# Rows of two, three and three batch elements in layer 1, and few-bit feed-forwards in halves

## The chip, the cores and the metric

The kernel runs on one core of one Trainium2 chip. A core has TensorE for matrix products, VectorE (DVE), ScalarE (ACT) and GpSimd (POOL) for everything elementwise, and SyncE (SP), whose queue issues nearly all DMAs here. Times are device microseconds of one execution; for a version the median of several executions counts, and less is better.

## The reference, cut to what matters

Two layers work on `x`, 8 batch elements of 512 tokens with 256 channels, and on a context of 512 tokens with 128 channels. Each layer adds to `x` a gated attention part and a gated feed-forward part, each on a normalised `x`.

- Layer 0, attention: causal self-attention and cross-attention over the context, 16 heads of 16 channels, then a projection.
- Layer 0, feed-forward: `h = gelu(qlinear(x, W1))`, `out = qlinear(h, W2)`, where `qlinear` quantises its input to 8 bits with one scale for the whole tensor. The second one needs the smallest and the largest `h` of all batch elements before any of them can go on.
- Layer 1, attention: two transformer blocks one after the other, `a1` (self-attention; the mask comes after the softmax and keeps keys later than the query) and `a2` (attention over the context). Both have 16 heads of 32 channels, and each has an MLP of its own, 256 to 1024 to 256:

```python
o = softmax(q k^T / sqrt(32)) (* mask) @ v
x_out = x + o @ li1_w + li1_b
h = gelu(_ln(x_out) @ li2_w + li2_b)
return x_out + h @ li3_w + li3_b
```

- Layer 1, feed-forward: activations quantised to 8 bits with a scale for each token, weights to three values, and between the two products a convolution over three tokens for each channel and a SiLU: `bit_linear(silu(conv(bit_linear(x, w1))), w2)`.

## The kernel before

Everything of batch element `b` stays with tokens or channels on the 128 partitions. The work is given out by a planner while the program is built. `Pace` (line 745) notes every instruction that is recorded, with a cost from a table (`cost`, line 863), and so keeps for each engine the time at which it should be free. The pieces of work are Python generators wrapped as `Stream`: each yields `need(...)`, the tiles that it waits for next, and whether its next piece starts on TensorE. [...]A helper records all matmuls on line 1022 and all transposes on line 1025.

Layer 0's attention, and its first feed-forward product, come first (up to about 910 us). What the second product needs is stored to memory: `hd`, 1 MB for each batch element. Layer 1 then is one long weave, `layer1_xattn` with `weave_all` (line 1762). Its parts:

- **Attentions** (`steps1`, line 2120): 16 of them, called slots here, in the order `order`. Before, the batch elements go in pairs: (0, a1), (1, a1), (0, a2), (1, a2), (2, a1), and so on. A slot has 4 head groups of 4 steps. A step's `front` makes the scores of four heads for 128 keys into two PSUM tiles `ps_s` and their exponentials into `pt` on ScalarE (line 2146); for a1, GpSimd selects the diagonal block into `dg` (line 2150). Its `back` multiplies with the values into the single bank `ov`. VectorE sums the exponentials into `acc` (lines 2175 and 2177). At the end of a group, VectorE turns the sums into reciprocals and scales `ov` into `oT` (lines 2190 to 2195), and only then can the next group's first `back` use `ov`. At most two fronts are ahead of the backs.
- **`pre1`** (line 1939): two normalisations in front of a1, the transposed `zT`, and the values `vt`. **`pair1`** (line 2011): queries and keys of one head group; for a2 the keys come from memory (`kd`), where they were put earlier.
- **`mlp1`** (line 2031): for each half of 256 tokens: output projection `li1`, normalisation, MLP with `li2`, Gelu (line 2093) and `li3`. After a1 its end prepares the same batch element's a2 (`enter1`). The half 0 of a1's MLP also loads a2's values into `vt` (line 2080).
- **`first`** (line 1856): the second product of layer 0's feed-forward, in two halves of 256 tokens: load `hF`, scale and round on ScalarE (line 1883), clip and subtract on VectorE (lines 1885 and 1887), 16 matmuls.
- **`last`** (line 2215): layer 1's feed-forward of one batch element, for which a2's MLP must be done. In each half, eight times: one product, `hp` (line 2249), then the convolution on `hF` (lines 2252 to 2261); then SiLU (line 2265), the largest magnitude of each token (`hm`, line 2269), a scale from it through two small TensorE groups, `hF*sr` and its rounding into `hq` (lines 2284 and 2286), 16 matmuls.
- **`tail`** (line 2315): the same feed-forward for the last batch element, each half by itself, with the convolution on TensorE.

Each stream has a `base`, the slot number at which it is due, and a `share`, by which its due time grows as its work gets done. `weave_all` takes, among the pieces that can start by the time TensorE should be free, the one that is due first. A piece that doesn't start on TensorE is recorded once its tiles are ready and VectorE's planned end is no more than `lag` ahead of TensorE. `first` and `last` form one list, sorted by base: `first` of the batch elements 0 to 7 is due at -1, 0, 1, 2, 3, 4, 7, 8, `last` of 0 to 6 at 5, 6, 9, 10, 13, 14, 15.

MLP weights have one buffer each. A new set is loaded when both halves of the second element of a pair have used the old one (`used`, line 1829), and a stream waits in `weight` until the set of its pair is in.

Of the kernel before, what the change touches and what calls it, by code (L numbers as in the profile page):

```python
# [8 lines left out]
F32 = mybir.dt.float32  # L9
BF16 = mybir.dt.bfloat16  # L10
AF = mybir.ActivationFunctionType
ALU = mybir.AluOpType
AX = mybir.AxisListType
PSUM = bass.MemoryType.PSUM

P = 128
B, T, C, CC = 8, 512, 256, 128
H = 16
NT = T // P
# [5 lines left out]

MAGIC = 12582912.0
NEG = -1.0e30
PTS = 3
KEYS_FIRST = 6

# [714 lines left out]
class Pace:  # L745
# [117 lines left out]
    def cost(self, e, ins, outs, srcs):  # L863
        size = self.size

        op = str(ins.opcode)
        n = max(size(a) for a in outs + (srcs if "Reduce" in op else []))

        few = sum(size(a) == 1 for a in srcs)
        if e == "PE":  # L870
            start = 0.0 if self.groups is None else 0.19
            if ins.is_transpose:
                return start + 0.095
            return start + n * (0.00169 if srcs[0].dtype == F32 else 0.00042)
        if e == "Activation":
            f = str(getattr(ins, "func", "Copy")).rsplit(".", 1)[-1]
            sbuf = srcs[0].tensor.space != PSUM
            t = n * 0.00084 + 0.16
            if f == "Identity":
                t += 0.22 if sbuf else 0.09 * few  # L880
            elif f == "Gelu" and n <= T:
                t += 0.19
            if f in ("Exp", "Gelu", "Silu") and f != self.table:
                self.table = f
                t += 1.28
            return t
        psum = any(a.tensor.space == PSUM for a in outs + srcs)
        two = sum(size(a) == n for a in srcs) > 1
        if e == "Pool":
            if "Affine" in op:  # L890
                return 0.25 + n * 0.001
            return 1.05 if n <= 2 * NT and two else 0.22 + n * 0.0021
        if "Reduce" in op:
            return 0.14 + n * (0.00173 if len(srcs[0].ap) > 2 and list(srcs[0].ap)[-1][0] > 1 else 0.00106)
        if "BNStats" == op:
            return 0.41
        if n <= 4 * NT:
            return 0.17
        if psum or two or "Transpose" in op:
            return 0.15 + 0.05 * few + n * 0.00106  # L900
        return 0.15 + 0.05 * few + n * 0.0006
# [2 lines left out]
WAIT = object()  # L904


def need(*tiles, pe=True, room=()):


    return [Pace.name(t) for t in tiles], pe, room  # L910


class Stream:
# [27 lines left out]
class Fast(General):  # L941
# [94 lines left out]
    def weave_timed(self, ops, streams, drain=False):  # L1036

        pace, behind = self.pace, self.behind  # L1040
        ops = list(ops)
        n_ops, i = len(ops), 0
        live = list(streams)

        def advance(s):
            w = pace.work
            s.need = next(s.gen, None)
            s.done += pace.work - w
            if s.need is None:
                s.over = True  # L1050
                if s in live:
                    live.remove(s)

        def starts(s):
            names, on_pe, room = s.need
            t = max([pace.when(names)] + [pace.place(tag) for tag in room])
            return max(t, pace.place("m1")) if on_pe else t

        while i < n_ops or live or (drain and not behind.over):
            now = pace.free.get("PE", 0.0)  # L1060
            cands = []
            for s in live + ([] if behind.over else [behind]):
                while s.need is WAIT:
                    last = s.need
                    advance(s)
                    if s.need is WAIT:
                        break
                while not s.over and s.need is not WAIT and not s.need[1] and starts(s) <= now:
                    advance(s)
                if s.over or s.need is WAIT:  # L1070
                    continue
                cands.append((s.base + s.share * s.done / s.total, starts(s), s))
            if i < n_ops:
                cands.append((i / n_ops, ops[i][0](), None))
            if not cands:
                continue
            can = [c for c in cands if c[1] <= now + 0.3]
            pick = min(can, key=lambda c: c[0]) if can else min(cands, key=lambda c: (c[1], c[0]))
            if pick[2] is not None:
                advance(pick[2])  # L1080
            else:
                ops[i][1]()
                i += 1
# [624 lines left out]
    def layer1_xattn(self):  # L1708
        nc, tc = self.nc, self.tc
        with (  # L1710
# [16 lines left out]

            self.pairs = self.fronts = self.backs = self.zTs = self.nvt = 0
            self.li1s, self.mlps, self.loads, self.both_in = [0, 0], [0, 0], {}, {}
            order = [(2 * p + k, blk) for p in range(B // 2) for blk in range(2) for k in range(2)]  # L1730
            few, pairs, mlps, pres = [], [], [[], []], [[], []]

            for k, b in zip((-1, 0, 1, 2, 3, 4, 7, 8), range(B)):
                few.append(Stream(self.first(b), 3.8, 0.8, k, 1.0))
                if b == 1:
                    few.append(Stream(self.load_mlp(), 1.0, 1.0, k))
            for k, b in zip((5, 6, 9, 10, 13, 14, 15), range(B - 1)):
                few.append(Stream(self.last(b), 10.5, 0.8, k, 1.0))
            few.sort(key=lambda s: s.base)
            for k, (b, blk) in enumerate(order):  # L1740
# [6 lines left out]
            for half in range(2):  # L1747
                mlps[half][-1].base += 0.4 * half
                mlps[half].append(Stream(self.tail(half), 20.0, 1.0, 17 + 0.4 * half))
            self.final, self.tails = {}, [0, 0]  # L1750
            diag = [Stream(self.diagonals(), 1.0, 0.1, 15.5)]
            self.keys_done, self.x0_read = False, 0
            keys = [Stream(self.keys2_rest(), 8.0 * (B - KEYS_FIRST), 1.0, -1.0)]
            self.weave_all(
                [self.steps1(b, blk) for b, blk in order], [few, pairs, *mlps, *pres, diag, keys]
            )
            self.pace.close()

# [3 lines left out]
    def weave_all(self, attns, chains):  # L1762
# [12 lines left out]
                c.pop(0)  # L1775

        def starts(s):
            names, on_pe, _ = s.need
            t = max(pace.when(names), pace.free["DVE"] - s.lag)
            return max(t, pace.place("m1")) if on_pe else t  # L1780

        while self.backs < len(steps) or any(chains):
# [39 lines left out]

    def weight(self, name, b, blk):

        while self.loads.get(name) != self.slot_of(b, blk) // 2:
            yield WAIT
        return self.wl[name]

    def used(self, name, b, blk):

        if self.both(b, (name, blk)) and b % 2 and (b, blk) != (B - 1, 1):
            self.next_weight(name, 1 - blk)

    def few_weights(self, layer, names):
# [21 lines left out]
    def first(self, b):  # L1856
# [22 lines left out]
        for half in range(2):  # L1879
            if half:  # L1880
                h = h2 or load_h(1)
            yield need(h, pe=False)
            nc.scalar.activation(h, h, AF.Identity, scale=self.rh, bias=self.magic)
            yield need(h, pe=False)
            nc.vector.tensor_scalar(h, h, self.hlo, self.hhi, ALU.max, ALU.min)
            hq = work.tile([P, NF, n], BF16, tag="hq", name="hq")
            nc.vector.tensor_scalar(hq, h, MAGIC, None, ALU.subtract)
            yield need(hq, x)
            ps = self.bank().rearrange("p (k c) -> p k c", k=2)
            for k in range(2):  # L1890
# [107 lines left out]

    def slot_of(self, b, blk):

        return 4 * (b // 2) + 2 * blk + b % 2

    def turned_half(self, z):

# [6 lines left out]
    def pair1(self, b, blk, g):  # L2011
# [15 lines left out]
            self.plus(KT, ps, w["wk_b"][:, g : g + 1])  # L2027
        q["QK", blk, g] = (QT, KT)
        self.pairs += 1

    def mlp1(self, b, blk, half):

# [37 lines left out]
        if blk:  # L2070
# [1 line left out]
            x = self.load_x(1, b, f"xo{half}", half)  # L2072
            yield need(res, x, pe=False)
            nc.vector.scalar_tensor_tensor(res, res, self.gate[:, 1:2], x, ALU.mult, ALU.add)
        elif not half:
            while self.nvt < self.slot_of(b, 1) or self.backs < 16 * (self.slot_of(b, 1) - 1):
                yield WAIT
            vt = q["vt", 1] = work.tile([P, NT, 2 * C], F32, tag="vt", name="vt", bufs=2)
            self.nvt += 1
            nc.sync.dma_start(vt.rearrange("p t c -> p (t c)"), self.vd[b])  # L2080
        li2 = yield from self.weight("li2", b, blk)
        h = work.tile([P, NF, n], F32, tag=f"hD{half}", name="hD")
        for f2 in range(NF // 2):
# [131 lines left out]
    def last(self, b):  # L2215
# [25 lines left out]
        for half in range(2):  # L2241
# [3 lines left out]
            for f in range(NF):  # L2245
# [14 lines left out]
                for k in (1, 2):  # L2260
                    nc.vector.scalar_tensor_tensor(  # L2261
                        a, hp[:, half + k : half + k + n], self.col("conv_w", 3 * f + k), a, ALU.mult, ALU.add
                    )
            yield need(h, pe=False)
            nc.scalar.activation(h, h, AF.Silu)
            yield need(h, pe=False)

            hm = work.tile([P, n], F32, tag="hm", name="hm")
            nc.vector.tensor_reduce(  # L2269
                hm, h.rearrange("p f t -> p t f"), AX.X, ALU.max, apply_absolute_value=True  # L2270
            )
            yield need(hm)
            ps = self.bank()[:, 0:n]
            for i in range(2):
# [5 lines left out]
            yield need(sc)  # L2280
            sr = work.tile([P, n], F32, tag="sr", name="sr")
            nc.scalar.copy(sr, self.row_of(sc, range(2)))
            yield need(sr, pe=False)
            nc.vector.tensor_tensor(h, h, sr.unsqueeze(1).to_broadcast([P, NF, n]), ALU.mult)
            hq = work.tile([P, NF, n], BF16, tag="hq", name="hq")
            nc.vector.tensor_scalar(hq, h, MAGIC, MAGIC, ALU.add, ALU.subtract)
            nc.vector.tensor_scalar(k, un, self.units["f1_w2"], self.gate[:, 3:4], ALU.mult, ALU.mult)
            yield need(hq, k, x)
            ps = self.bank().rearrange("p (k c) -> p k c", k=2)
# [236 lines left out]
```

## Time and profile before

Three executions took 2857.25, 2861.83 and 2867.59 us. The profile is of another execution.

| what | value |
|---|---|
| median of the three executions | 2861.83 us |
| profiled execution, its own time | 2859.76 us |
| its span, from the first to the last instruction | 2858.0 us |
| TensorE busy, matmuls | 2531.8 us (89%) |
| VectorE busy | 1708.6 us (60%) |
| ScalarE busy | 1453.9 us (51%) |
| GpSimd busy | 619.6 us (22%) |
| mean granted TensorE clock | 0.953 |
| moved by DMA | 181.79 MB, 64 GB/s |
| first score matmul of layer 1 | 964.1 us |
| last score matmul of layer 1 | 2695.4 us |

How to read it: the profile cuts the span into 40 equal slices and gives the busy share of each engine in tenths, and the clock that the throttle granted to TensorE. A row of a group has its line, engine, operation, the tiles it writes and reads, shape and count, its busy time and the mean duration in ns. A wait is put down to the instruction that ended it. Since matmuls overlap and their ends are modelled, a busy TensorE is not one that works at its peak.

### The profile page before, as it was taken

To read this page: it belongs to the slowest core of one execution; us is meant where nothing else is said; L and a number is where in the kernel's file an instruction comes from. 1 tells how busy PE (TensorE), PEld (TensorE's weight loads), DVE (VectorE), ACT (ScalarE), POOL (GpSimd) and SP (SyncE) were. 2 spreads that over 40 slices of the span, in tenths; PEclk is the share of its full clock that TensorE was granted. 3 is DMA by queue.
4 is the path that set the end of the run, shared out by engine and by line. 5 is a ranking of instruction groups with operands and counts; after the bars stand their busy time and mean duration, and the time that the engine had idled before them with its cause. 6 is when DMAs were issued, how large, how long until landed. Compare 5 with 4: busy or idle time off the path is not lost.

```text
span 2858.0 us, 38403 instructions
## 1 busy us (share of the span) xinstructions
PE 2531.8 (89%) x15431; PEld 1227.1 (43%) x15436; DVE 1708.6 (60%) x3014; ACT 1453.9 (51%) x1802; POOL 619.6 (22%) x693
## 2 busy tenths in 40 slices
PE   5999999999874888999999998999899999898875
PEld 2333333333232335445545444456354455353454
DVE  2434544344276555656656767766777755767766
ACT  3666666566574534544445544454554444554431
POOL 2112221121100333313332112132323112212010
PEclk9999999999987989999999999999999999998988
DMA  2011101100165421231220120131111020021010
GB/s 95 23 42 48 49 8 64 34 31 12 41 244 216 153 84 54 92 103 63 63 78 23 34 100 15 67 126 52 52 61 58 23 82 23 28 84 45 16 45 16
DMA packets 77338, 181.79 MB, mean 64 GB/s; under 512 B 7520, under 2 KB 36576, under 8 KB 69344
## 3 DMA queue, kind: packets, MB, share of 16 engines
q1 hardware_dynamic: 74768, 176.05, 17.6%
q8 instruction: 123, 2.02, 0.3%
q0 software_dynamic: 800, 2.62, 0.3%
q10 hardware_dynamic: 1584, 0.58, 0.1%
q14 instruction: 63, 0.52, 0.1%
HBM read 116.32 MB, written 62.91 MB: 63 GB/s over the span
## 4 chain that ended last, share of the span: by engine, by line
PE 67%; DVE 18%; ACT 7%; issue 4%; POOL 3%; DMA 1%; SPq 0%; ACTq 0%; POOLq 0%; DVEq 0%
PE ps L1022 38%; PE ps_s L1022 15%; PE ov L1022 12%; DVE hext L1636 2%; PE ps L1025 2%; ACT pt L1384 1%; POOL dg L2150 1%; DVE mv L1907 1%; ACT pt L2146 1%; DVE hF L2261 1%; DVE hm L2269 1%; DVE acc L2177 1%; DVE acc L2175 1%; DVE rb L2193 1%; ACT hD L2093 1%
## 5 line engine op out<-in xcount | busy, mean ns | idle before, releaser
L2146 ACT ACTIVATE pt<-ps_s 128x1024 f32<-128x1024 f32 x512 | 496.4, 1021 | 441.9 <-PE ps_s L1022 352.0
L1022 PE MATMUL ps_s<-QT,KT 32*128 32x512 f32 (+3 forms) x4096 | 618.0, 612 | 35.8 <-ACT pt L2146 12.2
L1384 ACT ACTIVATE pt<-ps_s 128x1024 f32<-128x1024 f32 (+3 forms) x512 | 411.6, 862 | 196.5 <-PE ps_s L1022 188.8
L1022 PEld LDWEIGHTS ps_s<-QT,KT 32*128 32x128 f32 x4096 | 193.7, 186 | 372.2 <-issue 202.0
L2150 POOL TENSOR_SCALAR_AFFINE_SELECT dg<-pt 128x512 f32<-128x512 f32 x128 | 121.3, 949 | 649.8 <-ACT pt L2146 649.7
L1022 PE MATMUL ov<-pt,v 128*32 128x512 f32 (+3 forms) x2048 | 235.3, 530 | 17.2 <-POOL pt L1387 14.1
L1022 PE MATMUL ps<-li,hD 128*128 128x256 f32 x1024 | 238.8, 389 | 12.1 <-ACT hD L2093 12.1
L1022 PE MATMUL ps<-x3T,li 128*128 128x256 f32 x1024 | 244.0, 390 | 1.4 <-ACT x3T L2063 1.1
L1022 PE MATMUL ov<-pt,vt 128*32 128x512 f32 (+3 forms) x1792 | 204.8, 525 | 39.4 <-DVE oT L2195 33.2
L1022 PEld LDWEIGHTS ps<-li,hD 128*128 128x128 f32 x1024 | 193.4, 193 | 66.1 <-issue 17.6
L1022 PEld LDWEIGHTS ps<-x3T,li 128*128 128x128 f32 x1024 | 192.0, 194 | 55.3 <-issue 15.3
L1387 POOL TENSOR_SCALAR_AFFINE_SELECT pt<-pt 128x512 f32<-128x512 f32 x128 | 86.4, 676 | 477.3 <-ACT pt L1384 477.3
L1913 POOL TENSOR_SCALAR mv<-mv 128x2 f32<-128x2 f32 (+1 forms) x105 | 51.2, 487 | 621.0 <-DVE mv L1908 560.9
L2177 DVE TENSOR_TENSOR acc<-acc,pt 128x2048 f32<-128x2048 f32 x64 | 151.9, 2374 | 8.2 <-ACT pt L2146 7.2
L2175 DVE TENSOR_TENSOR acc<-pt 128x2048 f32<-128x2048 f32 x64 | 149.7, 2339 | 0.6 <-ACT pt L2146 0.6
L1409 DVE STREAM_TRANSPOSE ot<-ov 128x512 f32<-128x512 f32 x64 | 45.8, 715 | 166.3 <-PE ov L1022 166.3
L1022 PE MATMUL ps<-zT,a_wq 128*128 128x512 f32 x256 | 135.4, 656 | 6.1 <-DVE zT L1994 4.1
L2261 DVE SCALAR_TENSOR_TENSOR hF<-hp,cols,hF 128x256 f32<-128x256 f32 x224 | 113.1, 505 | 34.6 <-ACT hF L2252 28.1
L1022 PE MATMUL ps<-li,oT 128*128 128x256 f32 x512 | 128.0, 395 | 1.6 <-DVE oT L2195 1.1
L1022 PEld LDWEIGHTS ov<-pt,v 128*32 128x32 f32 x2048 | 40.6, 108 | 174.9 <-issue 109.5
L1022 PEld LDWEIGHTS ps<-li,oT 128*128 128x128 f32 x512 | 94.0, 193 | 44.5 <-issue 16.4
L1025 PE MATMUL ps<-ident,z 128*128 128x128 f32 x328 | 60.9, 308 | 55.2 <-DVE z L137 34.5
(285 smaller groups left out, 3618.1 us busy)
## 6 DMA issues: line engine op xcount, KB each, us to landing
hd<-h SPq DMA_DIRECT2D x16, 1024.0 KB, 3.9
hF<-hd SPq DMA_DIRECT2D x16, 1024.0 KB, 6.7
li<-in_w_a_dram SPq DMA_DIRECT2D x16, 1024.0 KB, 5.0
fw<-q_f_w SPq DMA_DIRECT2D x22, 512.0 KB, 5.8
xF<-xd SPq DMA_DIRECT2D x22, 512.0 KB, 5.3
kd<-k SPq DMA_DIRECT2D x8, 1024.0 KB, 4.9
vd<-v SPq DMA_DIRECT2D x8, 1024.0 KB, 5.0
res<-rd SPq DMA_DIRECT2D x32, 256.0 KB, 2.7
```

The lines of the kernel that those rows point to most:

```text
L1022: self.nc.tensor.matmul(out, lhsT, rhs, start=start, stop=stop, skip_group_check=True)
L1025: self.nc.tensor.transpose(out, in_, self.ident)
L1384: nc.scalar.activation(pt[:, 2 * jp : 2 * jp + 2, lo:], pss[jp][:, :, lo:], AF.Exp)
L1387: nc.gpsimd.affine_select(out=diag, in_=diag, compare_op=ALU.is_ge, fill=0.0, base=0, pattern=[[0, 4], [1, P]], channel_multiplier=-1,)
L1409: nc.vector.transpose(ot.rearrange("p b d -> p (b d)"), ov)
L1636: nc.vector.tensor_reduce(e, hh, AX.X, op)
L1913: nc.gpsimd.tensor_scalar(rstd, mv[:, :, 1], EPS, None, ALU.add)
L2146: nc.scalar.activation(pt[:, 2 * jp : 2 * jp + 2, :], pss[jp], AF.Exp)
L2150: nc.gpsimd.affine_select(out=dg, in_=pt[:, :, diag], compare_op=ALU.is_gt, fill=0.0, base=0, pattern=[[0, 4], [-1, P]], channel_multiplier=1,
L2175: nc.vector.tensor_tensor(st["acc"], st["pt"], pt, ALU.add)
L2177: nc.vector.tensor_tensor(st["acc"], st["acc"], pt, ALU.add)
L2261: nc.vector.scalar_tensor_tensor(a, hp[:, half + k : half + k + n], self.col("conv_w", 3 * f + k), a, ALU.mult, ALU.add)
```

## The change

Three things are changed.

1. **Rows.** The pairs become the rows `ROWS`: (0, 1), (2, 3, 4) and (5, 6, 7). Each row runs a1 for all its elements and then a2 for all of them. So slots 0 to 5 stay as they are, ending with (2, a1) and (3, a1); then come (4, a1), (2, a2), (3, a2), (4, a2), (5, a1), (6, a1), (7, a1), (5, a2), (6, a2), (7, a2). `slot_of` and the weights' waits follow the rows; there are six sets of MLP weights to load in place of eight. The load of a2's values leaves `mlp1` and becomes the stream `values2`. The due times of `first` and `last` become `FIRST_AT` and `LAST_AT`.
2. **Pieces.** In `first`, the ScalarE operation and both VectorE operations are done in two halves of the 1024 channels. In `last`, `hm` is done in two halves of the tokens, and `hF*sr` and `hq` in two halves of the channels. Between two pieces the planner may record other work.
3. **Planner.** `need` can name the engine whose backlog holds a piece back: the ScalarE pieces of `first` and the SiLU of `last` now look at ScalarE's, not at VectorE's. The table's cost of a small fp32 matmul gets a lower limit of 0.22.

```diff
+ROWS = ((0, 1), (2, 3, 4), (5, 6, 7))
+FIRST_AT = (-1, 0, 1, 2, 4, 5, 7, 9)
+LAST_AT = (6, 7, 8, 11, 12, 13, 15)
...
-            return start + n * (0.00169 if srcs[0].dtype == F32 else 0.00042)
+            return start + max(0.22, n * 0.00169) if srcs[0].dtype == F32 else start + n * 0.00042
...
-def need(*tiles, pe=True, room=()):
+def need(*tiles, pe=True, room=(), on="DVE"):
...
-    return [Pace.name(t) for t in tiles], pe, room
+    return [Pace.name(t) for t in tiles], pe, room, on
...
-            order = [(2 * p + k, blk) for p in range(B // 2) for blk in range(2) for k in range(2)]
+            self.rows = [(blk, bs) for bs in ROWS for blk in range(2)]
+            order = self.order = [(b, blk) for blk, bs in self.rows for b in bs]
...
-            for k, b in zip((-1, 0, 1, 2, 3, 4, 7, 8), range(B)):
+            for k, b in zip(FIRST_AT, range(B)):
...
-            for k, b in zip((5, 6, 9, 10, 13, 14, 15), range(B - 1)):
+            for k, b in zip(LAST_AT, range(B - 1)):
...
+            vals = [Stream(self.values2(b), 1.0) for b, blk in order if blk]
...
         def starts(s):
-            names, on_pe, _ = s.need
-            t = max(pace.when(names), pace.free["DVE"] - s.lag)
+            names, on_pe, _, on = s.need
+            t = max(pace.when(names), pace.free[on] - s.lag)
...
-        while self.loads.get(name) != self.slot_of(b, blk) // 2:
+        while self.loads.get(name) != self.row_at(b, blk):
...
-        if self.both(b, (name, blk)) and b % 2 and (b, blk) != (B - 1, 1):
+        if self.both(b, (name, blk)) and b == self.rows[self.row_at(b, blk)][1][-1] and (b, blk) != (B - 1, 1):
             self.next_weight(name, 1 - blk)
...
-            yield need(h, pe=False)
-            nc.scalar.activation(h, h, AF.Identity, scale=self.rh, bias=self.magic)
-            yield need(h, pe=False)
-            nc.vector.tensor_scalar(h, h, self.hlo, self.hhi, ALU.max, ALU.min)
+            for f in (slice(0, NF // 2), slice(NF // 2, NF)):
+                yield need(h, pe=False, on="Activation")
+                nc.scalar.activation(h[:, f, :], h[:, f, :], AF.Identity, scale=self.rh, bias=self.magic)
             hq = work.tile([P, NF, n], BF16, tag="hq", name="hq")
-            nc.vector.tensor_scalar(hq, h, MAGIC, None, ALU.subtract)
+            for f in (slice(0, NF // 2), slice(NF // 2, NF)):
+                yield need(h, pe=False)
+                nc.vector.tensor_scalar(h[:, f, :], h[:, f, :], self.hlo, self.hhi, ALU.max, ALU.min)
+                nc.vector.tensor_scalar(hq[:, f, :], h[:, f, :], MAGIC, None, ALU.subtract)
...
-        return 4 * (b // 2) + 2 * blk + b % 2
+        return self.order.index((b, blk))
+
+    def row_at(self, b, blk):
+
+        return next(i for i, (k, bs) in enumerate(self.rows) if k == blk and b in bs)
...
+    def values2(self, b):
+
+        at = self.slot_of(b, 1)
+        while self.nvt < at or self.backs < 16 * (at - 1) or not self.keys_done:
+            yield WAIT
+        vt = self.seqs[b]["vt", 1] = self.work.tile([P, NT, 2 * C], F32, tag="vt", name="vt", bufs=2)
+        self.nvt += 1
+        self.nc.sync.dma_start(vt.rearrange("p t c -> p (t c)"), self.vd[b])
...
-        elif not half:
-            while self.nvt < self.slot_of(b, 1) or self.backs < 16 * (self.slot_of(b, 1) - 1):
-                yield WAIT
-            vt = q["vt", 1] = work.tile([P, NT, 2 * C], F32, tag="vt", name="vt", bufs=2)
-            self.nvt += 1
-            nc.sync.dma_start(vt.rearrange("p t c -> p (t c)"), self.vd[b])
...
-            yield need(h, pe=False)
+            yield need(h, pe=False, on="Activation")
             nc.scalar.activation(h, h, AF.Silu)
-            yield need(h, pe=False)
...
-            nc.vector.tensor_reduce(
-                hm, h.rearrange("p f t -> p t f"), AX.X, ALU.max, apply_absolute_value=True
-            )
+            for i in range(2):
+                yield need(h, pe=False)
+                t2 = slice(i * P, (i + 1) * P)
+                nc.vector.tensor_reduce(
+                    hm[:, t2], h[:, :, t2].rearrange("p f t -> p t f"), AX.X, ALU.max, apply_absolute_value=True
+                )
...
-            yield need(sr, pe=False)
-            nc.vector.tensor_tensor(h, h, sr.unsqueeze(1).to_broadcast([P, NF, n]), ALU.mult)
             hq = work.tile([P, NF, n], BF16, tag="hq", name="hq")
-            nc.vector.tensor_scalar(hq, h, MAGIC, MAGIC, ALU.add, ALU.subtract)
+            for f in (slice(0, NF // 2), slice(NF // 2, NF)):
+                yield need(sr, pe=False)
+                nc.vector.tensor_tensor(
+                    h[:, f, :], h[:, f, :], sr.unsqueeze(1).to_broadcast([P, NF // 2, n]), ALU.mult
+                )
+                nc.vector.tensor_scalar(hq[:, f, :], h[:, f, :], MAGIC, MAGIC, ALU.add, ALU.subtract)
```

## The prediction

> **What bounds the kernel now.** I read the slices of the whole span first, then stretches cut at the first score matmul of each layer-1 attention, then the waits of TensorE, then the groups that the change touches. From the page:
>
> ```profile
> PE   5999999999874888999999998999899999898875
> DVE  2434544344276555656656767766777755767766
> PEclk9999999999987989999999999999999999998988
> ```
>
> TensorE is 90% busy or more in most slices; VectorE and ScalarE have room on average. So only what stands between matmuls can be saved. The 16 attentions of layer 1 ("slots" 0 to 15, in the order in which they run) begin at 964.1 us, the last score matmul starts at 2695.4, the end is at 2858.0. Busy time of the engines in some of these stretches (us, busy PE, PEld, DVE, ACT, POOL, granted clock, DMA):
>
> ```profile
> 1262.60:1364.00 101.40, 100.56 (x565) 50.20 (x564) 60.65 (x96) 49.58 (x54) 24.69 (x21) 1.00 0.20 68
> 1471.20:1586.20 115.00, 104.76 (x677) 58.73 (x676) 76.04 (x130) 54.76 (x64) 30.49 (x35) 0.93 0.08 29
> 2695.40:2858.00 162.60, 108.36 (x506) 80.11 (x502) 106.75 (x210) 45.79 (x77) 12.21 (x19) 0.84 0.08 27
> ```
>
> The first (slot 3) has no `last` feed-forward in it and no idle TensorE; the second (slot 5) has one. The third, the tail after the attentions, is 162.6 us, with TensorE idle for a third of it.
>
> A busy TensorE can still be late: I took for each kind of matmul group in layer 1 the lower quartile of start to next start (scores of four heads 1.07 us, four 128x256 groups of `li2` 1.73, one `li3` tile 3.45) as its undisturbed price. Slots 0 to 15 then hold 1480 us of such work in 1732 us, so 252 us are stalls: 46 in slots 0 and 1, 4 in slot 3, 8 in slot 4, 16 on average in slots 5 to 15. The tail holds 85 us of it in 162.6: 77 us of stalls. Who TensorE waits for, slots 0 to 15, then the tail (us, times, longest):
>
> ```profile
> PE ov L1022 <- DVE oT L2195: 33.2, 22, 4.9
> PE ov L1022 <- POOL dg L2150: 19.0, 13, 5.6
> PE ps L1025 <- DVE z L137: 11.5, 11, 2.4
> PE ps L1022 <- ACT hD L2093: 9.0, 6, 2.6
> PE ps L1025 <- ACT z L1919: 8.1, 7, 2.8
> PE ps L1025 <- DVE hm L2269: 6.4, 3, 4.0
> ...
> PE ps L1025 <- DVE hm L2269: 10.2, 3, 6.5
> PE ps L1025 <- DVE z L2331: 7.3, 2, 6.2
> PE ps L1022 <- DVE hq L2286: 6.5, 3, 3.7
> ```
>
> No line is a DMA; the largest is the softmax scaling `oT`, which frees the one `ov` bank.
>
> [...] PEclk is 1.00 in slot 3, 0.93 in slot 5, 0.84 in the tail[...] L1883 measures 2.09, which I use.
>
> **The change, part by part.** *Pieces.* The operations that are cut, as they are now (ns minimum, median, maximum; first and last start):
>
> ```profile
> L1883 ACT ACTIVATE hF<-hF,magic,qh_rs x16: 2082/2093/2097, 917.3 to 1926.8; 128x2048 f32<-128x2048 f32 x16
> L1885 DVE TENSOR_SCALAR hF<-hF,qh_lo,qh_hi x16: 1314/1337/2152, 919.4 to 1929.0; 128x2048 f32<-128x2048 f32 x16
> L2269 DVE TENSOR_REDUCE hm<-hF x14: 3583/3712/3783, 1554.0 to 2815.7; 128x256 f32<-128x2048 f32 x14
> L2284 DVE TENSOR_TENSOR hF<-hF,sr x14: 2283/2293/2642, 1572.4 to 2822.9; 128x2048 f32<-128x2048 f32 x14
> ```
>
> Added: 16 ACT activations[...]; on VectorE 16+16+14+14+14 = 74 instructions[...], over 1900 us in which VectorE is idle a third: nothing on the path[...]. Removed: the longest block in front of a short operation falls from 3.71 to 1.85 (`hm`)[...]. In slots 0 to 15, 47 of the 252 us of stalls have such an operation running in them or ending at most 1 us before. Half of that would be the most. But a cut only helps where something is put between: in the new order 9 of 14 pairs of `hm` have other work between them, 4 of 14 of `hF*sr`, 7 of 16 of the clip. So about half the pairs, half the block: 47 x 0.2 = 9 us saved; bounds 0 and 24. ScalarE's long pieces now are held back by ScalarE's own backlog instead of VectorE's: part of the same.
>
> *Rows.* A slot's MLP and second normalisation must be done before the second attention of that batch element, two slots later before, three in the new rows. TensorE's work is the same instructions (9318), reordered. I counted, in both orders, the undisturbed TensorE work that stands between a group and the one that needs its result through other engines, against the time the trace gives for that path: `oT` 0.71+0.25+0.71+0.69 and hand-overs 2.6 us; `z` after `li1` 3.9 (add, statistics 1.2, POOL 0.9, scaling 0.7); Gelu 3.6 (0.47+1.28+1.90); the `hF*sr` path 4.2; `hm` 7.5; its scales 1.4; `x3T` 1.1. What is missing, summed over slots 0 to 15, before and after: `oT` 24.8, 17.0; `z` 10.9, 2.6; Gelu 15.7, 10.2; `x3T` 4.9, 3.2; `hm` 2.2, 2.2; scales 0, 1.7; `hF*sr` 1.3, 0. Total 59.8 to 36.9: 23 us saved. The remaining stalls (POOL's `dg`, exponentials, half clock) I hold constant. Bounds: 0, if other streams already stood in those gaps late; 50, if the half clock goes down with them.
>
> *DMAs.* Eight sets of MLP weights become six: six loads fewer, 5 MB. TensorE waits for none of them (no such line), so 0. The value load `vt` leaves the MLP for a stream of its own; on the SP queue it waits for its buffer, with `KT`, `res` and `rd` transfers behind it. A `vt` lands in 5.8 us, a slot takes about 108, and `KT` is fetched a head group (27 us) ahead: 0, and a few us if a `KT` is late.
>
> *FIRST_AT, LAST_AT.* Slot 0 gets two half feed-forwards of layer 0 in place of three (three 16-matmul groups to two). VectorE work between `oT`s of one slot: its peaks are 90.7 and 90.2 us before, 98.7 (slot 8) and 96.8 (slot 11) after, beside 92 and 105 us of TensorE work. Before, 90.7 and 88.4 went with slots of 111.6 and 116.3 us, so I give these no gain.
>
> *Tail.* `last(5)` can only follow the attention of (5,1), slot 13 rather than 11. Its second half now runs into the tail: five of its eight column steps (hp, two multiply-adds, about 1.5 us each) move there. VectorE's work after the last `acc` rises from 109.3 to 118.9 us, all by counted instructions. The missing time, counted as above, rises from 45.9 to 52.3. `last(6)` begins after the last MLP's `li3` groups instead of among them, some 11 us later; against that the last tail half then overlaps with `last(6)`, where now it stands alone for 22 us (2831 to 2853). I take +7; bounds -8 and +20.
>
> Sum on the profiled execution: span 2858.0 - 9 - 23 + 7 = 2833. The median of the runs shown is 3.8 above the span (2861.8), so 2837.
>
> **Rivals.** (1) VectorE becomes the bound in the full slots: in slots 8 and 11 at the ratio of slot 6 (111.6/90.7 = 1.23) VectorE's 98.7 and 96.8 us make 121 and 119 us, against 106 for the mean of 16 slots less the gain: 28 us, which eat the 32 us of pieces and rows. For it: VectorE has the largest waits of TensorE; against: slot 11 of before, with 84.7 us, took only 101. Then 2862 - 32 + 7 + 28 = 2865: no change. (2) Slower: the tail. If VectorE sets it, 9.6 us more work and the later start of `last(6)` (11) add up to 20 us; it decides as soon as rows and pieces save less than 20. With 5 saved, 2877. For it: VectorE is busy 107 of 162.6 us there; against: half of the tail's wait is latency, not load. (3) More: [...] By the clock's records slots 0 to 15 have 130 us at half clock, worth up to 65; if half of these windows go, 30 us more, 2807. For it: slots 3, 4 and 10 have none, and stalls of 4, 8 and 9 us. Against: [...] most gaps are short and stay.
>
> **How the numbers follow.** Likeliest (2820 to 2853): 0.50, at 2837. Rival 3: 0.20. Rival 1: 0.16. Rival 2: 0.14. A difference under 0.3% (8.6 us) cannot be told from no change here. Faster 0.50 + 0.20 = 0.70; same 0.16; slower 0.14. The range takes in most of rival 3 and of rival 1 and leaves out rival 2's upper half: 2804 to 2872; the likeliest alone, 2820 to 2853.
>
> **What would show it.** TensorE's waits for `oT` under 27 us and for `z` under 12 in the slots; granted clock above 0.955; no stretch of layer 1 over 118 us; the stretch after the last score matmul 165 to 175 us, with `last(5)` in it. Wrong if the slots between 6 and 12 don't get shorter, or the tail grows by over 12 us.

## The result, and the profile after

The changed kernel takes **2835.22 us** (median of 4 executions, 2829.34 to 2836.92) against 2860.45 us (2857.25 to 2867.59): a ratio of **0.9905**, interval 0.9881 to 0.9929. Forecast: 2837. The profiled execution took 2834.51 us, with a span of 2832.7.

From the page of the changed kernel, VectorE, TensorE and the granted clock in 40 slices:

```profile
PE   5999999999874889899999989998999989999875
DVE  3434544444277556555655776777776877777766
PEclk9999999999987999999999999999999999999987
```

From slice 23 to the end VectorE is now busy 6 tenths or more in every slice; before, it fell to 5 in two of them. The dips of TensorE lie in other places, but there are still dips. Stretches again cut at the first score matmul of each attention: slot 9 before, then slots 5 and 9 and the tail of the changed kernel (us; busy PE, PEld, DVE, ACT, POOL; clock; DMA):

```profile
1927.70:2035.80 108.10, 98.28 (x672) 54.47 (x671) 76.17 (x141) 56.72 (x68) 34.57 (x39) 0.97 0.14 50
1461.50:1567.30 105.80, 102.40 (x685) 56.65 (x684) 65.50 (x123) 49.66 (x56) 43.51 (x45) 1.00 0.15 51
1883.90:2009.50 125.60, 114.02 (x596) 58.13 (x596) 89.66 (x161) 56.21 (x69) 19.66 (x22) 0.92 0.12 40
2659.10:2832.70 173.60, 115.79 (x514) 84.30 (x512) 116.91 (x238) 46.96 (x77) 11.65 (x19) 0.79 0.08 25
```

Slot 5 went from 115.0 us at clock 0.93 to 105.8 at 1.00; slot 9, which holds (5, a1) before and (4, a2) after, grew from 108.1 to 125.6; the tail grew from 162.1 to 173.6. With the prices of the prediction, this is where the time went in the two profiled executions (us; stalls are my own count, which no view shows; half clock is the time in which the clock's records show half):

| | before | after |
|---|---|---|
| layer 1 begins at | 964.1 | 962.8 |
| slots 0 to 15, length | 1731.8 | 1696.3 |
| of it stalls | 252.2 | 217.8 |
| stalls in slots 0-2, 3-5, 6-12, 13-15 | 59.4, 33.8, 98.9, 60.1 | 57.9, 15.2, 112.9, 31.8 |
| half clock in slots 0 to 15 | 129.7 | 88.7 |
| tail, length (half clock in it) | 162.1 (52.8) | 173.6 (72.6) |

Who TensorE waits for, slots 0 to 15, then the tail (us, times, longest):

```profile
PE ov L1025 <- DVE oT L2210: 26.6, 19, 3.0
PE ps_s L1025 <- ACT pt L2161: 25.6, 33, 3.0
PE ps L1028 <- DVE z L140: 14.9, 14, 3.0
PE ov L1025 <- POOL dg L2165: 9.0, 9, 3.4
...
PE ps L1025 <- DVE hq L2402: 7.6, 2, 4.1
PE ps L1025 <- DVE hq L2306: 6.1, 5, 2.0
PE ps L1028 <- DVE z L2351: 6.1, 2, 3.7
PE ps L1028 <- DVE hm L2286: 5.1, 4, 1.7
```

`oT` fell from 33.2 to 26.6 and `dg` from 19.0 to 9.0. But `z` on VectorE rose from 11.5 to 14.9, and the second line is new at this size: the scores wait for exponentials, 25.6 us where it was 12.2 (`PE ps_s L1022 <- ACT pt L2146: 12.2, 25, 1.0` in the kernel before). The shares of the change are not to be seen from these two profiles; the experiments below take them apart.

### The profile page after: what moved, and what is told of

Its sections match the earlier page's. It is cut to its first block, busy times and chain, and to the rows that moved or that the text cites. A ratio compares the mean times of both kernels' runs of the same rounds, so it can differ in the third digit from the quotient of the medians.

```text
span 2832.7 us, 38465 instructions
## 1 busy us (share of the span) xinstructions
PE 2527.3 (89%) x15436; PEld 1226.2 (43%) x15436; DVE 1717.0 (61%) x3073; ACT 1461.6 (52%) x1825; POOL 618.3 (22%) x693
## 4 chain that ended last, share of the span: by engine, by line
PE 66%; DVE 18%; ACT 7%; issue 4%; POOL 3%; DMA 1%; SPq 0%; ACTq 0%; POOLq 0%; DVEq 0%
PE ps L1025 38%; PE ps_s L1025 15%; PE ov L1025 12%; DVE hext L1639 2%; ACT pt L2161 2%; PE ps L1028 2%; ACT pt L1387 1%; DVE hF L2276 1%; DVE acc L2190 1%; DVE mv L1915 1%; POOL dg L2165 1%; DVE z L140 1%; DVE rb L2208 1%; DVE acc L2192 1%; DVE rt L2205 1%
## 5 line engine op out<-in xcount | busy, mean ns | idle before, releaser
L1025 PE MATMUL ps_s<-QT,KT 32*128 32x512 f32 (+3 forms) x4096 | 619.5, 609 | 45.8 <-ACT pt L2161 25.6
L1025 PE MATMUL ov<-pt,vt 128*32 128x512 f32 (+3 forms) x1792 | 203.1, 523 | 33.0 <-DVE oT L2210 26.6
L2165 POOL TENSOR_SCALAR_AFFINE_SELECT dg<-pt 128x512 f32<-128x512 f32 x128 | 110.2, 862 | 519.5 <-ACT pt L2161 519.3
L1921 POOL TENSOR_SCALAR mv<-mv 128x2 f32<-128x2 f32 (+1 forms) x105 | 60.4, 575 | 744.9 <-DVE mv L1916 692.1
L1025 PE MATMUL ps<-zT,a_wq 128*128 128x512 f32 x256 | 129.2, 629 | 1.4 <-DVE zT L2002 0.8
L1703 ACT ACTIVATE hD<-ps,cols 128x256 f32<-128x256 f32 x126 | 56.5, 472 | 138.9 <-PE ps L1025 97.6
```

Of the source, the lines that this page charges most:

```text
L1025: self.nc.tensor.matmul(out, lhsT, rhs, start=start, stop=stop, skip_group_check=True)
L1703: self.nc.scalar.activation(out, ps, AF.Identity, bias=bias)
L1921: nc.gpsimd.tensor_scalar(rstd, mv[:, :, 1], EPS, None, ALU.add)
L2165: nc.gpsimd.affine_select(out=dg, in_=pt[:, :, diag], compare_op=ALU.is_gt, fill=0.0, base=0, pattern=[[0, 4], [-1, P]], channel_multiplier=1,
```

## The experiments

My theory was the prediction's: rows give most, pieces a little, and the tail gives some back. The rivals were VectorE as the bound of the full slots, the half clock as the real carrier, and the planner or the due times as the real source. All kernels were timed against the kernel before, in four groups at different times; its medians there were 2860.45, 2860.42, 2861.61 and 2861.16 us. The ratio is against the kernel before of the same group. Stalls and half clock are those of one profiled execution of each kernel.

| kernel | median us | ratio, interval | slots: stalls, half clock | tail, half clock |
|---|---|---|---|---|
| changed | 2835.22 | 0.9905, 0.9881 to 0.9929 | 217.8, 88.7 | 173.6, 72.6 |
| rows_only | 2835.35 | 0.9913, 0.9893 to 0.9933 | 213.2, 99.0 | 178.4, 76.0 |
| pieces_only | 2856.25 | 0.9987, 0.9974 to 1.0001 | 241.5, 105.8 | 167.1, 53.0 |
| pairs_after | 2851.59 | 0.9961, 0.9943 to 0.9980 | 241.6, 105.8 | 167.1, 53.0 |
| no_planner | 2847.72 | 0.9961, 0.9950 to 0.9973 | 234.2, 112.6 | 172.9, 64.1 |
| no_on | 2846.60 | 0.9941, 0.9920 to 0.9961 | 230.6, 102.4 | 172.8, 64.0 |
| rows_332 | 2843.64 | 0.9956, 0.9941 to 0.9971 | 231.4, 78.5 | 171.6, 64.2 |
| old_due | 2880.68 | 1.0058, 1.0040 to 1.0076 | 262.4, 109.2 | 175.4, 71.3 |
| old_last | 2843.21 | 0.9943, 0.9922 to 0.9964 | 230.5, 102.4 | 172.8, 67.6 |
| due_only | 2892.27 | 1.0116, 1.0090 to 1.0143 | 269.6, 122.9 | 176.6, 75.5 |
| dose | 2859.29 | 0.9992, 0.9978 to 1.0006 | 239.7, 88.7 | 171.8, 65.0 |
| warm_tail | 2823.20 | 0.9864, 0.9845 to 0.9883 | 215.2, 88.7 | 167.1, 32.2 |
| warm_plus | 2825.28 | 0.9880, 0.9855 to 0.9904 | 214.9, 78.5 | 167.0, 32.0 |

### Rows alone, pieces alone

`rows_only` is the changed kernel with the pieces, `on=` and the price floor taken back; rows, `values2` and the new due times stay. `pieces_only` is the kernel before with the pieces and `on=`:

```diff
 # rows_only, in first (and so in last)
-            for f in (slice(0, NF // 2), slice(NF // 2, NF)):
-                yield need(h, pe=False, on="Activation")
-                nc.scalar.activation(h[:, f, :], h[:, f, :], ...)
+            yield need(h, pe=False)
+            nc.scalar.activation(h, h, ...)
```

> Rows, values2 and the new due times alone; first and last uncut, the planner as before. Theory A (the order gives the gain, as in the prediction: 23 us from rows, 9 from pieces, tail +7): about 2845 us, tail longer than 165 us. Rival B (the cut pieces give the gain): 2858 to 2866, the tail costs what little the order brings. Rival C (the plan is touchy, any change of order moves some 10 us either way): anywhere in 2840 to 2870, and the waits for z and oT do not follow the counts.

> The cut operations of first and last, held back by the backlog of the engine they run on, in the old pairs with the old due times. Theory A: 2851 us (9 less than before), tail within 5 us of 162. Rival B: 2835 to 2842. Rival C: 2840 to 2870.

The rows (with their due times) carry all of the gain that can be seen, 10 us more than expected for them; pieces alone bring 4 us, with an interval that includes none. Together they bring no more than the rows alone, but the two ratios and their intervals leave some 11 us of gain to 7 us of loss for the pieces on top of the rows. Inside the profiled executions, `rows_only` has 39 us fewer stalls in the slots than before and a tail 16 us longer; with the pieces on top, stalls in the slots are 5 us more and the tail is 5 us shorter. The waits of TensorE in the slots say what each does ("..." marks lines left out). First `rows_only`, then `pieces_only`:

```profile
PE ov L1025 <- DVE oT L2208: 29.5, 18, 4.9
...
PE ps_s L1025 <- ACT pt L2159: 15.3, 24, 2.4
...
PE ps L1028 <- DVE z L140: 5.2, 7, 1.2
```

```profile
PE ps_s L1022 <- ACT pt L2148: 27.7, 30, 3.0
PE ov L1022 <- DVE oT L2197: 23.6, 16, 4.1
...
PE ps L1025 <- DVE z L137: 11.6, 10, 2.4
```

The rows take `z` from 11.5 to 5.2 and leave exponentials at 15.3. The pieces take `oT` from 33.2 to 23.6 and bring exponentials from 12.2 to 27.7. That shorter operations stand in the way of `oT` on VectorE, and ScalarE's pieces in the way of the exponentials, fits this but was not followed from instruction to instruction. In the other kernels of the table it is the same: with pieces 25 to 34 us of waits for exponentials, without (`rows_only`, `due_only`) 14 to 15. What a piece costs, in the changed kernel (ns minimum, median, maximum):

```profile
L1890 ACT ACTIVATE hF<-hF,magic,qh_rs x32: 1225/1239/1269, 916.0 to 2159.3; 128x1024 f32<-128x1024 f32 x32
L2286 DVE TENSOR_REDUCE hm<-hF x28: 1858/1913/2018, 1643.1 to 2802.5; 128x128 f32<-128x1024 f32 x28
L2303 DVE TENSOR_TENSOR hF<-hF,sr x28: 1210/1219/2284, 1663.2 to 2810.5; 128x1024 f32<-128x1024 f32 x28
```

The durations of two of ScalarE's add up to 2.48 us where one whole was 2.09. In 9 of the 16 pairs the second follows at once and starts 1.13 to 1.15 us after the first, so some 0.1 us before its end; from the first start to the second end these take 2.36 to 2.37 us. A cut then costs 0.28 us. By durations, two of `hm` make 3.83 for 3.71, two of `hF*sr` 2.44 for 2.29.

In the tail, TensorE meets the cut `hm` like this (start and duration in us; the wait before it in brackets):

```profile
2756.61 0.31 PE L1028 MATMUL ps<-ident,hm 128*128 128x128 f32 x1 [0.57 <-DVE hm L2286]
2758.63 0.33 PE L1028 MATMUL ps<-ident,hm 128*128 128x128 f32 x1 [1.72 <-DVE hm L2286]
```

Both transposes are recorded together after both halves, so TensorE begins the first and then stands for the second half, with the next matmuls behind it. One long wait became shorter ones with nothing put between: in the tail of `rows_only` the waits for the uncut `hm` are 5.9 us, the longest 5.5; here they are 5.1 us, the longest 1.7.

### Without the planner's part, and the planner's part split

```diff
 # no_on: every  on="Activation"  dropped; no_planner: the floor of 0.22 too
-            yield need(h, pe=False, on="Activation")
+            yield need(h, pe=False)
```

> The changed kernel without the planner's part: backlog of VectorE for every piece, no lower limit of a matmul's cost. Theory A and rival B: same as the changed kernel within 0.4%, 2826 to 2846. Rival C: 10 us or more away from it with no wait that explains it.

> The changed kernel with the 0.22 us floor of the planner's price for an fp32 matmul, but with the backlog of VectorE, not ScalarE, holding back the pieces on ScalarE. Without both settings the time was 2847.7 and slot 11 took 149.9 us, with 27 us at half clock. If the backlog rule made that slot long, it is again over 140 us and the time 2843 to 2850; if the price floor did, 2832 to 2839 and slot 11 near 122.

Both are 11 to 13 us slower than the changed kernel (`no_planner` just outside the expected 2826 to 2846), so it is `on=` that returns them. The price floor changes the order in layer 0 only: in the traces `no_on` and `no_planner` have one order in layer 1. The place is slot 11, here of `no_on` (121.9 us in the changed kernel):

```profile
2111.90:2261.70 149.80, 131.32 (x786) 73.86 (x786) 102.94 (x193) 66.81 (x82) 55.30 (x58) 0.91 0.19 64
```

It is longer partly because more work stands in it (113.8 us at the undisturbed prices, against 104.9), partly by stalls: 36 us, 27 at half clock.

### Old pairs with all the rest

`pairs_after` has `ROWS = ((0, 1), (2, 3), (4, 5), (6, 7))` and the old due times; pieces, planner and value stream stay.

> The changed kernel with the old pairs of batch elements and the old due times; pieces, the planner's two settings and the value stream stay. Rows alone gave 0.9913, pieces alone 0.9987. If the gain is the rows' (a batch element's second attention three slots after its first instead of two), almost all of it goes: 2853 to 2860 us, slots 0 to 15 with 238 us or more of stalls, waits for oT back to 30 us or more. If the planner's settings carry a part of their own, 2845 or less.

2851.59: a little better than expected, with 241.6 us of stalls as expected, but `oT` waits of 23.7 us rather than 30 or more: those are the pieces' work, not the rows'. Its layer 1 has the same order on TensorE, VectorE and ScalarE as `pieces_only` (2856.25), so a comparison of two kernels from different groups may be off by about 5 us. Pieces in pairs bring 4 to 10 us.

### Rows of three, three and two

> The changed kernel with rows (0,1,2), (3,4,5), (6,7): the feed-forward last(5) can follow slot 11 again instead of slot 13. If the longer tail (173.6 us after the last score matmul against 162.1) comes from last(5) running into it: tail 160 to 166, slots 0 to 15 within 10 us of the changed kernel's, total 2823 to 2830. If it comes from the pieces or from last(6) starting later: tail 170 to 176, total 2830 to 2840.

`ROWS = ((0, 1, 2), (3, 4, 5), (6, 7))` gave 2843.64. The forecast of a shorter tail failed: 171.6 us. VectorE still has 115.3 us of work there (116.9 in the changed kernel, 106.3 before), so the last feed-forwards still run into it: `LAST_AT` still has `last(5)` due at 13, and 4 of its 16 steps `hp` lie in the tail, where the changed kernel has 5 and the kernel before none. So this run did not take `last(5)` out of the tail, and what the tail would be without it stays open. Slots 1 and 7 took 126 us each.

### The due times

```diff
 # old_due: both lists old, rows as changed; old_last: this one alone
-LAST_AT = (6, 7, 8, 11, 12, 13, 15)
+LAST_AT = (5, 6, 9, 10, 13, 14, 15)
 # old_due
-FIRST_AT = (-1, 0, 1, 2, 4, 5, 7, 9)
+FIRST_AT = (-1, 0, 1, 2, 3, 4, 7, 8)
```

> The changed kernel with the old FIRST_AT and LAST_AT, rows as changed. If the due times are worth nothing by themselves, as forecast: 2832 to 2840 us. If the gain is in where the few-bit feed-forwards stand (slots 4, 5, 7 and 9 instead of 3, 4, 7 and 8; last ones in 6, 7, 8, 11, 12, 13, 15), half of it goes: 2845 to 2855.

> The changed kernel with the old LAST_AT alone, FIRST_AT as changed. If the 45 us lie in where the last feed-forwards stand: 2865 to 2882 us, slots 10 and 11 near 130 us. If they lie in the first ones (no first one in slots 7 and 8 ahead of them in the one chain that they share): 2832 to 2845.

> The kernel before with the new FIRST_AT and LAST_AT alone: old pairs, no pieces, old planner. With the rows the new due times were worth 45 us (2880.7 with the old ones). If they are worth that only because the rows move the moment from which a last feed-forward can run, here they give nothing or cost: 2855 to 2875 us. If they are better in themselves, 2825 to 2845.

This was the surprise. Rows with the old due times are **slower than before** (2880.7), the new due times in the old pairs (`due_only`: the kernel before with the two lists) slower still (2892.3); both lie outside everything that was expected. Only rows and due times together gain. Old `LAST_AT` alone costs 8 us, so with the old `LAST_AT` in place 37 us (33 by the ratios) hang on three entries of `FIRST_AT`: elements 4, 5 and 7 a slot later. The old `FIRST_AT` beside the new `LAST_AT` was not run. Of these 37, 28 lie in slots 3 to 6. Slots 5 and 6 in `old_due`, then in `old_last`:

```profile
1466.90:1585.50 118.60, 108.94 (x703) 60.07 (x702) 88.25 (x164) 58.06 (x72) 42.25 (x47) 0.99 0.07 23
1585.50:1706.40 120.90, 104.43 (x678) 58.87 (x678) 83.52 (x150) 56.05 (x69) 31.95 (x38) 0.93 0.13 46
```

```profile
1457.30:1565.40 108.10, 103.97 (x681) 57.18 (x680) 66.20 (x125) 50.27 (x57) 45.28 (x47) 0.98 0.15 50
1565.40:1676.30 110.90, 100.70 (x681) 57.11 (x680) 84.96 (x154) 56.98 (x70) 40.21 (x40) 0.95 0.10 34
```

With `first` of elements 4 and 5 done a slot early, `last(0)` moves into slot 5 (10 of its 16 steps `hp` run there, in `old_last` none; VectorE 88.3 us instead of 66.2), and slot 6 follows it with 83.5: two full slots in a row, with 16 and 28 us of stalls against 9 and 17. Over all slots the waits for `z` on VectorE are 21.5 us in `old_due` and 9.8 in `old_last`, those for exponentials 34.3 and 26.9. Beyond that the stops are spread over many short waits, and I did not take them further apart.

### Does VectorE bound the full slots?

```diff
 # dose: in back(), for slot >= 3 and the first two steps of a head group
+            if n < 2 and slot >= 3:
+                nc.vector.tensor_reduce(self.dose, self.ident[:, 0:1].to_broadcast([P, T]), AX.X, ALU.max)
```

> The changed kernel with two extra operations of about 0.7 us on VectorE in each head group of slots 3 to 15 (5.5 us a slot, 71 us in all; their result is read by nobody). If VectorE is the bound of the full slots (9 to 12, 85 to 90 us of VectorE work each), these four grow by 6 to 9 us each, the slots with 55 to 70 us by under 2, and the time by 30 us or more. If the stalls there are chains of short dependent operations, the growth is even over the slots and small: 8 to 18 us in all.

Slot 10, in the changed kernel and then in `dose`:

```profile
2009.50:2126.80 117.30, 107.86 (x727) 61.05 (x726) 89.18 (x147) 62.06 (x75) 19.16 (x23) 0.99 0.13 41
2004.50:2121.50 117.00, 106.47 (x711) 58.61 (x710) 98.16 (x159) 59.28 (x68) 18.89 (x23) 1.00 0.12 41
```

70.2 us of extra work on VectorE (104 at 0.675) cost 24 us, more than forecast for short chains and less than for a bound. It did not gather in the full slots: slot 10 held 9 us more VectorE work and took no longer, slots 9 to 12 together grew by 7.4 us (117.6, 117.0, 135.1, 114.8 against 125.6, 117.3, 121.9, 112.3), all 13 dosed slots by 21.5 in this execution, so the four took about their share. Since the planner knows the extra cost, the order moved too, and a slot's growth isn't the extra work alone. This speaks against VectorE as the bound of those slots, but its time is not free either: about 0.3 us for each microsecond over the whole of this run, an estimate (24 of 70.2).

### Is the tail longer because of the clock?

```diff
 # warm_tail: extra matmuls ahead of the waits in the tail
+        for i in range(n):     # n = 4, 6 or 12, once all attentions are done
+            self.mm(self.final["dum"][:, i % 2, :], w[:, 0, 0:P], w[:, 0, 0:T])
 # warm_plus: in tail(), by halves of the tokens
+            nc.vector.tensor_tensor(h[:, :, t2], h[:, :, t2], sr[:, t2]..., ALU.mult)
+            nc.vector.tensor_scalar(hq[:, :, t2], h[:, :, t2], MAGIC, MAGIC, ALU.add, ALU.subtract)
```

> The changed kernel with extra bf16 matmuls 128x512 (4 to 12 at a time, results not read, into a bank of the scores that is free by then) put ahead of the matmuls that wait for z, hm, sc2 and hq after the last attention. If the tail is longer because TensorE runs at half clock there (72.6 us of it, against 52.8 before), half clock falls under 45 us, the stretch after the last score matmul goes from 173.6 to 158 to 165 us and the time to 2820 to 2828. If VectorE's chain sets the tail, the clock rises and the time doesn't change (2832 to 2838), or grows by the few us that the extra matmuls stand in the way.

> The kernel with extra matmuls in the tail, and there the multiplication by sr7 and the rounding to hq7 in two halves of 128 tokens, so that the first 8 of 16 matmuls start while VectorE does the second half. By the tail's waits for hq (1.3 to 4 us, two times) at most 3 us: 2819 to 2824 us; if the strided halves cost VectorE what the overlap gives, 2822 to 2826.

The tail of `warm_tail`, and the extra matmuls:

```profile
2653.30:2820.40 167.10, 125.38 (x606) 86.50 (x604) 116.77 (x238) 46.52 (x77) 11.65 (x19) 0.90 0.08 26
L1025 PE MATMUL dum<-fw x92: 377/379/634, 2685.3 to 2812.3; 128*128 128x512 bf16 x92
```

TensorE is given 92 useless matmuls (23 us busy), and the tail is shorter: 167.1 us against 173.6 (158 to 165 forecast), with VectorE's work unchanged (116.8) and half clock at 32.2 us in place of 72.6. So half clock does cost time here: 40 us less of it gave 6.5 us back, what the extra matmuls cost already taken off. That is not yet 6.5 of the 11.5 us by which the tail grew, for half clock now lies below the 52.8 us of the kernel before. At the same rate, the 20 us by which it had risen are some 3 us, an estimate. The larger part of the growth has another cause; the 10.7 us of VectorE work that moved there is the candidate, not shown by itself. The rest of the 12 us by which this kernel is faster lies before the tail, where the order of work is the same; that much is scatter. At 2823.2 us this version is faster than both kernels. Halves in the tail (`warm_plus`, with 8 extra matmuls for 12 ahead of `hq7`) add nothing.

## Why the prediction was right or wrong, point by point

**Total: right (2837 forecast, 2835.22 measured), in part by luck.** Rows with their due times bring the gain and the tail gives part back, as forecast. But errors in the terms cancelled. `rows_only` has 39 us fewer stalls in the slots, where 23 was the step, and a tail 16 us longer, where 7 was. In the changed kernel the slots are 35.5 us shorter (32 forecast for rows and pieces together) and the tail 11.5 us longer. And the gain needed the new due times, to which the sum gave nothing.

**Pieces, -9: not found.** In pairs 4 to 10 us; on top of the rows no gain was measured (2835.35 without, 2835.22 with), though the intervals don't exclude one of 9. The step that failed is "half the pairs, half the block": it priced the stalls that go, and not what the shorter pieces displace. In `pieces_only` the waits for exponentials are 15.5 us longer than before and those for `oT` 9.6 us shorter, and without `on=` the pieces would have cost 11 to 12 us. The product was also rounded down: half of half of 47 is 12, and 0.23 (20 of 44 pairs, half the block) gives 11. VectorE's busy time rose by 8.4 us (1708.6 to 1717.0), and hidden altogether it was not: at the rate of `dose` it costs about 3 us, an estimate.

**Rows, -23: too small, and mixed in its terms.** `rows_only` against before, by the same groups and prices (my own count; no view shows it): `z` 19.8 to 10.1 (forecast -8.3), Gelu 12.0 to 7.3 (-5.5), `x3T` 11.1 to 8.7 (-1.7): these hold. The largest term, `oT` -7.8, fails: 73.5 to 72.3 for the group that opens `ov`. In its place came gains that were not in the sum: the queries' projection 14.0 to 4.6, `hm` 10.6 to 6.0, and less half clock, 129.7 to 99.0. Holding the clock constant was a mistake: in the changed kernel the slots have 41 us less at half clock. In its trace the 128x256 matmuls of `li2` start 216 ns apart at full clock and 427 ns apart at half (medians, my own count), so the 41 us are worth at most half of that, 20 of the 34 us of stalls saved. The waits for `dg` were held constant too: 17.9 us in `rows_only` (19.0 before), but 9.0 in the changed kernel and 12.3 in `pieces_only`, so their gain goes with the pieces.

**FIRST_AT, LAST_AT, no gain: wrong.** They are worth 45 us given the rows, and cost 31 without them. The sum survived since the step on rows was counted on the order with both. It could not have been told by that count: made again, it gives 44.7 us of missing time in `old_due` and 51.7 in `due_only`, below the 59.8 of before, yet both are slower. The count sees each path for itself; two full streams at once on one engine, as in slots 5 and 6 of `old_due`, are not in it.

**DMAs, 0: right.** In layer 1 of the changed kernel no wait of TensorE was ended by a DMA.

**Tail, +7: right in kind, +11.5 in size.** Five steps `hp` of `last(5)` lie in the tail, as counted, and VectorE's work there rose by 10.7 us (forecast 9.6). Missed was the clock: half clock rose from 52.8 to 72.6 us, worth some 3 us by the estimate above.

**Rival 1, VectorE the bound:** its long slots came (125.6 and 121.9 us with 89.7 and 89.6 us of VectorE work; forecast 121 and 119 for two such slots), but `dose` speaks against VectorE as their bound, and the other slots fell by more. **Rival 2** didn't decide. **Rival 3** came in part: a third of the half clock went, not half. It does not carry the gain by itself: `rows_332` has less half clock in the slots (78.5 us) than the changed kernel and is 8 us slower, and `old_due` has less (109.2) than the kernel before and is 20 us slower than it.

**The signs named.** `oT` under 27: 26.6, yes, though the rows alone leave 29.5. `z` under 12: 14.9, no, though 5.2 with the rows alone. Clock above 0.955: 0.955, no. No stretch over 118: no, slots 9 and 11. Tail 165 to 175: 173.6, yes. "Wrong if the slots between 6 and 12 don't get shorter": they grew, 777.6 to 793.7 us; the gain lies in slots 3 to 5 (-17) and 13 to 15 (-34). By that sign the place was wrong, though the two kinds of attention both stall less (a1 141 to 119 us, a2 111 to 99), since the rows change which attention has which number. The tail grew by 11.5, just under the 12 named; in `rows_only` it grew by 16.

## What to carry to other kernels

Where a planner weaves streams, an order and the due times of what is woven in are one parameter: try them together, and count no gain or loss for one of them alone. Cutting long operations can move waits instead of removing them: in `pieces_only` the waits for `oT` fell by 9.6 us and those for exponentials grew by 15.5. Look at what the pieces may stand in front of on their own engine, ScalarE's exponentials here. In a stretch that ends in dependent chains, look at the granted clock: 92 matmuls that nobody reads, put ahead of the waits, raised the tail's clock from 0.79 to 0.90 and took 6.5 us off it here.

## What the runs showed of the hardware that was not expected

The clock stayed low in the tail while TensorE was mostly busy. From 2736.2 to 2753.3 us of the changed kernel it was at half for 17.07 us on end, while TensorE was busy 77% of the time and after the first 0.4 us, the end of a wait of 3.75, no wait was longer than 1.4 us:

```profile
2736.20:2753.25 17.05, 13.05 (x42) 8.96 (x43) 12.46 (x30) 6.37 (x10) 0.00 (x0) 0.50 0.00 1
```

The clock's records of this execution (my own count; no view shows it) have 41 stretches at half clock. Of these, 40 last 3.41 us or a whole multiple of it, up to five times; the last one runs past the end of the span. Cut into five parts of 3.41 us, the stretch above has TensorE idle for 0.80, 1.61, 1.10, 0.50 and 0.00 us, with the ends of matmuls as the profile models them: full clock came back after the part without a gap, and the part with a single gap of 0.50 us was still at half clock.

The clock also fell with no long wait just before. Of the 26 stretches at half clock from the start of the changed kernel's layer 1, 23 began with no wait as long as 3.41 us in the 6.83 us before them; the one at 1811.2 us began after waits of at most 1.0 us. So the lower mean clocks in slot 5 and in the tail, which the prediction gives, don't show what length of wait brings the half clock. What share of busy time holds or releases the clock, these traces don't settle.
